# Four pre-normalised layers on one core: output projection woven into the last pair of heads, group means taken off X for good

## Chip, core and metric

The kernel is one program on one core of a Trainium2 chip. The metric is the device time of one execution, in microseconds (us). Everything is computed in float32.

## What is computed

X has 512 channels of 64 x 64 pixels (4096). Four layers follow one another, each reading the group-normalised X (32 groups of 16 channels, no scale or shift) and adding its result to X itself:

```python
x = x + L0(gn(x)); x = x + L1(gn(x)); x = x + L2(gn(x)); x = x + L3(gn(x))
def gn(v):                 # per group of 16 channels, over channels and pixels
    return (v - mean) / sqrt(var + 1e-5)
def L0(f):                 # 8 heads of 64 channels, all 4096 x 4096 scores
    q, k, v = (conv1x1(f, w / sqrt(512)) for w in (wq, wk, wv))
    sim = -(|q_i|^2 + |q_j|^2 - 2 q_i.k_j) / 8
    return conv1x1(softmax(sim) @ v, wo / sqrt(512))
def L1(f):                 # L2 is the same with other weights
    pwa, abc = split(conv1x1(f, w_in) + b_in, [128])   # 128 and 896 channels
    dw0, dw1, dw2 = split(depthwise7x7(abc) + dw_b)    # 128, 256, 512
    h = pwa * dw0
    h = (conv1x1(h, pw0) + b) * dw1
    h = (conv1x1(h, pw1) + b) * dw2
    return conv1x1(h, w_out) + b_out
def L3(f):                 # linear attention
    qkv0 = conv1x1(f, w_qkv) * s_qkv + b_qkv           # 768 channels
    agg = affine(depthwise5x5(qkv0))
    q, k, v = split(concat(qkv0, agg)); q, k = relu(q) + eps, relu(k) + eps
    y = (v k^T) q / (mean(k).q + eps) * g_norm + bt_norm + v
    return conv1x1(y, w_proj) * s_proj + b_proj
```

## The kernel before

X stays in SBUF all through, as four chunks of 128 channels (c = 0 to 3), and the 4096 pixels are worked on in eight blocks of 512 columns (b or k). The kernel issues its instructions through a framework that orders them per engine from its own estimates of time; each engine then runs its own list in order, with semaphores between the engines. In the convolution layers the matmuls (`pc.matmul`, line 579) keep the order in which they are written.

**Group parameters.** `_group_params` (L91) turns the per-block statistics (`bn_stats`) into mean and 1/std: four `bn_aggr` (L96), a small matmul with `gmask` (L98) that averages over a group, a copy of the mean (L100), three small operations, a second matmul (L107), Sqrt on ScalarE (L111), and five more small operations on VectorE that end in `gn_r` (L119).

**L0, `_attention_pairs`.** `_normalize` (L315) rewrites X as (X - mean) / std with 32 VectorE operations (L326), one per chunk and block. Then the heads go in four pairs. `project` makes Q, K and V of a pair (L394, L405). For each block of queries, 32 steps t follow: `scores` (four matmuls on quarters of the array, then two Exp on ScalarE), and, two steps behind, `values` (four matmuls) and an addition to `acc` on VectorE (L500). `close` divides a finished block by its sums (L462 to L475) and overwrites Q of that pair with the result; it is issued inside the next block at t = 3. All PSUM products except `av` rotate through three buffers (`ps_s`).

**The check and the output projection, `_attention`.** The kernel checks that all softmax sums were in range (`good`, `one`, `okay`, L510 to L513), every engine loads that value into a register (L524), and a branch (L525) skips a long general form of the attention, which does not run with these inputs. Since X was overwritten by its normalised form, the output projection loads the original X again (`xin`, L538), multiplies by `wo` (256 matmul instructions, L542; each fp32 matmul counts as two), adds (L545) and takes the statistics of the next layer (L548).

**L1 and L2, `_gated_convs`.** The weights are multiplied by 1/std in place (`scaled`, L740). The mean is not taken off X: the first time that a weight tile is used (`k == 0`), `taking` multiplies it with the mean as well (L761, `ps_m`, a product one column wide), and the result is taken off the bias (`b_in`, L764). Each product goes through VectorE into a zero-padded `plane` (L771) and from there, by a DMA that ScalarE triggers (L603), to DRAM (`F`), from where the depthwise convolution loads it shifted (`S`, L629).

**L3, `_linear_attention`.** It treats the mean in the same way (L963, `b_qkv`, L966 and L967); here ScalarE writes the plane (L970) and triggers the DMA.

Of the kernel before, what the change touches and what calls it, by code (L numbers as in the profile page):

```python
# [10 lines left out]
FP = mybir.dt.float32  # L11
# [5 lines left out]
P = 128  # L17
# [72 lines left out]

def _group_params(nc, small, psum, stats, gmask):  # L91


    mv = small.tile([P, NC, 2], FP, tag="gn_mv", name="gn_mv")
    for c in range(NC):
        nc.vector.bn_aggr(mv[:, c, :], stats[:, c, :, :].rearrange("p b s -> p (b s)"))  # L96
    ps = psum.tile([P, BLK], FP, tag="mm", name="gn_ps")
    nc.tensor.matmul(ps[:, 0:NC], gmask, mv[:, :, 0], start=True, stop=True)  # L98
    mean = small.tile([P, NC], FP, tag="gn_mean", name="gn_mean")
    nc.vector.tensor_copy(mean, ps[:, 0:NC])  # L100

    d = small.tile([P, NC], FP, tag="gn_d", name="gn_d")
    nc.vector.tensor_sub(d, mv[:, :, 0], mean)
    nc.vector.tensor_mul(d, d, d)
    nc.vector.tensor_add(d, d, mv[:, :, 1])
    ps = psum.tile([P, BLK], FP, tag="mm", name="gn_ps")
    nc.tensor.matmul(ps[:, 0:NC], gmask, d, start=True, stop=True)  # L107
    a = small.tile([P, NC], FP, tag="gn_a", name="gn_a")
    nc.vector.tensor_scalar(a, ps[:, 0:NC], GN_EPS, None, ALU.add)  # L109
    s = small.tile([P, NC], FP, tag="gn_s", name="gn_s")  # L110
    nc.scalar.activation(s, a, AF.Sqrt)  # L111
    r = small.tile([P, NC], FP, tag="gn_r", name="gn_r")
    nc.vector.reciprocal(r, s)

    t = small.tile([P, NC], FP, tag="gn_t", name="gn_t")
    nc.vector.tensor_mul(t, r, r)
    nc.vector.tensor_mul(t, t, a)
    nc.vector.tensor_scalar(t, t, -0.5, 1.5, ALU.mult, ALU.add)
    nc.vector.tensor_mul(r, r, t)  # L119
    return mean, r  # L120
# [3 lines left out]
def trunk_kernel(ctx: ExitStack, tc: tile.TileContext, a: dict, out: bass.AP):  # L124
# [42 lines left out]
    def new_stats():  # L167
        return small.tile([P, NC, NB, 6], FP, tag="stats", name="stats")

    dram = ctx.enter_context(tc.tile_pool(name="dram", bufs=1, space=bass.MemoryType.DRAM))  # L170
    F = [dram.tile([P, FORM.planes, FORM.plane], FP, tag=f"F{i}", name=f"F{i}") for i in range(NDW)]
# [5 lines left out]

    stats = _attention(tc, a, X, vcol, ident, gmask, neg2, small, new_stats)
    stats = _gated_convs(tc, a, X, vcol, gmask, small, new_stats, stats, F)
    _linear_attention(tc, a, X, vcol, vall, ident, gmask, small, stats, F3, Z, out)  # L180


# [131 lines left out]

def _normalize(tc, X, gmask, small, psum, new_stats):  # L315

    nc = tc.nc
    st = new_stats()
    for b in range(NB):
# [14 lines left out]

def _attention_pairs(tc, a, X, QO, gmask, small, new_stats, okay):

# [11 lines left out]
    scale = D ** -0.5  # L348
    gain_in = 1.0 / math.sqrt(C)
    NT = N // P  # L350
# [3 lines left out]
    with tc.tile_pool(name="att1", bufs=1) as p1, tc.tile_pool(  # L354
# [10 lines left out]

        ps_mm = _Halves()
        _normalize(tc, X, gmask, small, ps_mm, new_stats)


# [12 lines left out]
        def project(pair):  # L382
            w = p1.tile([P, 3, NC, P], FP, tag="wqkv", name=f"wqkv{pair}")
            nc.sync.dma_start(out=w, in_=a["L0_wqkv"][pair])
            Q = QO[pair]
            sq = []
            for b in range(NB):
                cols = ts(b, BLK)
                if b % 2 == 0:
                    sq.append(ptp.tile([P, 2 * BLK], FP, tag="pt", name="sq"))  # L390
# [71 lines left out]
        def close(pair, b, av, acc):  # L462
# [12 lines left out]
            nc.vector.scalar_tensor_tensor(good, rd, 1.0 / SUM_LOW, good, ALU.is_le, ALU.mult)  # L475

        for pair in range(HEADS // 2):
            project(pair)
            done = None
            for b in range(NB):  # L480
# [23 lines left out]
                nc.vector.tensor_add(avs, avs, av[1])  # L504
                done = (pair, b, avs, acc)
            close(*done)


# [6 lines left out]

def _attention(tc, a, X, vcol, ident, gmask, neg2, small, new_stats):

    nc = tc.nc
    gain_out = 1.0 / math.sqrt(C)
    opool = tc.alloc_tile_pool(name="opool", bufs=1, side="right")  # L520
    O = [opool.tile([P, N], FP, tag=f"O{i}", name=f"O{i}") for i in range(NC)]
    okay = small.tile([1, 1], mybir.dt.int32, tag="okay", name="okay")
    _attention_pairs(tc, a, X, O, gmask, small, new_stats, okay)
    found = nc.values_load(okay[0:1, 0:1])  # L524
    with tc.If(found < 1):  # L525
        _attention_general(tc, a, X, O, ident, neg2)

    stats = new_stats()
    with tc.tile_pool(name="wo", bufs=1, side="right") as wop, tc.tile_pool(
        name="xin", bufs=2, side="right"  # L530
    ) as xinp, tc.tile_pool(name="ps_o", bufs=4, space=PSUM) as ps_o:
        wo = wop.tile([P, NC, C], FP, tag="wo", name="wo")
        nc.scalar.dma_start(out=wo, in_=a["L0_wo"])
        for b in range(NB):
            cols = ts(b, BLK)
            xin = xinp.tile([P, NC, BLK], FP, tag="xin", name="xin")
            for c in range(NC):
                nc.sync.dma_start(out=xin[:, c, :], in_=a["x"][c, :, cols])  # L538
            for o in range(NC):
                ps = ps_o.tile([P, BLK], FP, tag="o", name="ps_o")  # L540
                for c in range(NC):
                    nc.tensor.matmul(  # L542
                        ps, wo[:, c, ts(o, P)], O[c][:, cols], start=(c == 0), stop=(c == NC - 1)
                    )
                nc.vector.scalar_tensor_tensor(  # L545
                    X[:, o, cols], ps, gain_out, xin[:, o, :], ALU.mult, ALU.add
                )
                nc.vector.bn_stats(stats[:, o, b, :], X[:, o, cols])  # L548
    opool.release()
    return stats  # L550
# [155 lines left out]
@with_exitstack  # L706
def _gated_convs(ctx, tc, a, X, vcol, gmask, small, new_stats, stats, F):

# [11 lines left out]
    for layer in ("L1", "L2"):  # L720
# [13 lines left out]
        nc.sync.dma_start(out=pw1, in_=a[f"{layer}_pw1"])  # L734
        mean, rstd = _group_params(nc, small, ps_mm, stats, gmask)
        stats = new_stats()
        b_in = small.tile([P, 8], FP, tag="b_in", name="b_in")

# [13 lines left out]

        def taking(w, i, k):


            ps = product(lambda c: w[:, c, :], [pc.pixels(X[:, c, :], k) for c in range(NC)])
            if k == 0:
                pm = ps_mm.tile([P, BLK], FP, tag="mm", name="ps_m")
                for c in range(NC):
                    pc.matmul(  # L760
                        pm[:, 0:1], w[:, c, :], mean[:, c : c + 1],  # L761
                        start=(c == 0), stop=(c == NC - 1),
                    )
                nc.vector.tensor_sub(b_in[:, i : i + 1], vcol(pre + "b_in", i), pm[:, 0:1])  # L764
            return ps

        def fused(i, k):

            pc.take(
                i, k, taking(w_in[i], 1 + i, k),  # L770
                lambda dst, src: nc.vector.tensor_scalar(  # L771
                    dst, src, b_in[:, 1 + i : 2 + i], None, ALU.add
                ),
# [6 lines left out]
        def gate(i, b):  # L780

            h = [D[c][:, ts(b, BLK)] for c in range(min(i, 3))]
            if i == 0:
                ps = taking(w_gate, 0, b)
                bias = b_in[:, 0:1]
            elif i < 3:
# [73 lines left out]
@with_exitstack  # L860
def _linear_attention(ctx, tc, a, X, vcol, vall, ident, gmask, small, stats, F, Z, out):

# [48 lines left out]
    with ExitStack() as st:  # L911
# [25 lines left out]

        mean, rstd = _group_params(nc, small, ps_mm, stats, gmask)

        def product(w, hs):  # L940
# [3 lines left out]
            return ps  # L944

        b_qkv = wp.tile([P, NQKV], FP, tag="b_qkv", name="b_qkv")

# [6 lines left out]
        def fused(i, k):  # L954

            w = w_qkv[i]
            ps = product(lambda c: w[:, c, :], [pc.pixels(X[:, c, :], k) for c in range(NC)])
            bias = b_qkv[:, i : i + 1]
            if k == 0:
                pm = ps_mm.tile([P, BLK], FP, tag="mm", name="ps_m")  # L960
                for c in range(NC):
                    pc.matmul(
                        pm[:, 0:1], w[:, c, :], mean[:, c : c + 1],  # L963
                        start=(c == 0), stop=(c == NC - 1),
                    )
                nc.vector.tensor_mul(bias, pm[:, 0:1], vcol(pre + "s_qkv", i))  # L966
                nc.vector.tensor_sub(bias, vcol(pre + "b_qkv", i), bias)  # L967
            pc.take(
                i, k, ps,
                lambda dst, src: nc.scalar.activation(  # L970
                    dst, src, AF.Identity, bias=bias, scale=vcol(pre + "s_qkv", i)
                ),
# [95 lines left out]
        def added():  # L1068
# [10 lines left out]
            nc.vector.tensor_mul(pbias, ps[:, 0:NC], vall(pre + "s_proj"))  # L1079
            nc.vector.tensor_add(pbias, pbias, vall(pre + "b_proj"))  # L1080


# [195 lines left out]
```

## Time and profile before

| | us |
|---|---|
| median of 3 runs | 3992.67 (3990.71 to 3994.23) |
| the profiled execution, its own time | 3995.15 |
| its span in the profile | 3993.1 |
| TensorE (PE) busy | 3896.0 |
| VectorE (DVE) busy | 2268.5 |
| ScalarE (ACT) busy | 1823.8 |
| GpSimd (POOL) busy | 66.7 |

A line of the profile names the source line, the engine, the operation, the tile written and the tile read, and how often it ran. PEld is the loading of weights into the array. "Idle before" is the time in which the engine stood still just before, with the engine or DMA that ended the wait. Start times are counted from the start of the span; 2.05 us of the execution lie outside it.

### The profile page before, as it was taken

How to read it: one execution, taken by the hardware profiler on the slowest of the kernel's cores; microseconds unless marked ns; L12 is line 12 of the kernel's file. 1: busy time of each engine (PE TensorE's matmuls, PEld its weight loads, DVE VectorE, ACT ScalarE, POOL GpSimd, SP SyncE). 2: the span in 40 equal slices, each digit the busy share in tenths (PEclk: the TensorE clock that was granted, in tenths of full speed). 3: DMA queues.
4: the chain of work that ended last, by engine and by line, in shares of the span. 5: the costliest groups of instructions: out<-in, count | busy, mean ns of one | idle time of the engine just before them, and what ended most of it. 6: DMA issues, size and time to landing. Idle time of an engine off the chain costs nothing. (4 is left out here: it accounts for less than half of the span.)

```text
span 3993.1 us, 81533 instructions
## 1 busy us (share of the span) xinstructions
PE 3896.0 (98%) x35842; PEld 1766.7 (44%) x35842; DVE 2268.5 (57%) x2497; ACT 1823.8 (46%) x2599; POOL 66.7 (2%) x67
## 2 busy tenths in 40 slices
PE   6999999999999999999998999999999999989999
PEld 4533346333353333543332445554455544445544
DVE  4677763777727777457776323466434664233335
ACT  0677753777717777357775024441144520222210
POOL 0000000000000000000000000000000000001110
PEclk9999999999999999999999999999999999989999
DMA  2000000000000000000000235551255511686234
GB/s 93 9 1 1 1 1 9 1 1 1 1 9 1 1 1 1 1 1 1 1 1 24 95 129 158 174 146 43 90 149 176 158 45 56 177 208 139 74 89 144
DMA packets 243097, 241.26 MB, mean 60 GB/s; under 512 B 15384, under 2 KB 204056, under 8 KB 242480
## 3 DMA queue, kind: packets, MB, share of 16 engines
q1 hardware_dynamic: 215920, 176.16, 16.4%
q10 hardware_dynamic: 26784, 59.76, 4.1%
q8 instruction: 284, 4.65, 0.5%
q14 instruction: 77, 0.63, 0.1%
q0 software_dynamic: 32, 0.06, 0.0%
HBM read 176.15 MB, written 59.77 MB: 59 GB/s over the span
## 5 line engine op out<-in xcount | busy, mean ns | idle before, releaser
L447 ACT ACTIVATE pt<-ps_s,A 128x512 f32<-128x512 f32 x2048 | 1286.7, 687 | 470.0 <-PE ps_s L439 451.6
L500 DVE TENSOR_TENSOR acc<-acc,pt 128x1024 f32<-128x1024 f32 x960 | 1174.3, 1223 | 334.3 <-ACT pt L447 308.3
L457 PE MATMUL av<-pt,V 64*64 64x512 f32 x8192 | 1116.5, 590 | 0.9 <-ACT pt L447 0.9
L439 PE MATMUL ps_s<-O,K 64*64 64x512 f32 x8192 | 1115.2, 589 | 0.0
L457 PEld LDWEIGHTS av<-pt,V 64*64 64x64 f32 x8192 | 343.0, 133 | 551.0 <-issue 509.7
L439 PEld LDWEIGHTS ps_s<-O,K 64*64 64x64 f32 x8192 | 338.7, 133 | 545.6 <-issue 286.2
L635 ACT COPY S<-S 32x1295 f32<-32x1295 f32 x224 | 284.2, 1269 | 353.1 <-DMA S<-F 285.9
L579 PE MATMUL ps<-X,w_in_L 128*128 128x512 f32 x896 | 407.0, 604 | 4.6 <-DVE w_in_L L740 4.6
L579 PE MATMUL ps_cv<-S,T 64*32 64x128 f32 x13824 | 242.5, 278 | 16.8 <-DMA S<-G 15.0
L579 PEld LDWEIGHTS ps_cv<-S,T 64*32 64x32 f32 x13824 | 199.5, 107 | 122.5 <-issue 80.8
L579 PEld LDWEIGHTS ps<-X,w_in_L 128*128 128x128 f32 x896 | 165.5, 191 | 197.2 <-issue 194.8
L771 DVE TENSOR_SCALAR plane<-ps,b_in 128x512 f32<-128x512 f32 x112 | 83.8, 748 | 263.7 <-PE ps L579 210.7
L394 PE MATMUL ps_qk<-X,wqkv 128*128 128x512 f32 x512 | 227.7, 598 | 2.1 <-DVE X L326 2.1
L579 PE MATMUL ps<-h,w_out_L 128*128 128x512 f32 x512 | 227.9, 598 | 0.0
L579 PE MATMUL ps<-X,w_qkv 128*128 128x512 f32 x384 | 172.7, 606 | 3.2 <-DVE w_qkv L949 3.2
L579 PE MATMUL ps<-h,pw_L 128*128 128x512 f32 x320 | 146.7, 610 | 7.4 <-DVE X L809 6.2
L398 ACT ACTIVATE O<-ps_qk 128x512 f32<-128x512 f32 x32 | 19.1, 597 | 277.5 <-PE ps_qk L394 277.5
L394 PEld LDWEIGHTS ps_qk<-X,wqkv 128*128 128x128 f32 x512 | 95.7, 192 | 113.1 <-issue 109.4
L579 PEld LDWEIGHTS ps<-h,w_out_L 128*128 128x128 f32 x512 | 95.0, 190 | 114.6 <-issue 106.5
L111 ACT ACTIVATE gn_s<-gn_a 128x4 f32<-128x4 f32 x4 | 0.8, 205 | 304.8 <-DVE gn_a L109 304.8
L830 ACT ACTIVATE h<-h,vec 128x1024 f32<-128x1024 f32 x56 | 63.0, 1147 | 154.6 <-DVE h L695 154.3
L689 DVE STREAM_TRANSPOSE h<-ps_cv 128x512 f32<-128x512 f32 x112 | 109.0, 1045 | 38.4 <-PE ps_cv L579 38.4
(130 smaller groups left out, 2486.4 us busy)
## 6 DMA issues: line engine op xcount, KB each, us to landing
T<-in_L_T_dram SPq DMA_DIRECT2D x112, 384.0 KB, 4.2
F<-plane ACTq DMA_DIRECT2D x112, 324.0 KB, 2.9
S<-F SPq DMA_DIRECT2D x224, 162.0 KB, 4.3
S<-G SPq DMA_DIRECT2D x192, 136.0 KB, 4.1
row<-G SPq DMA_DIRECT2D x80, 272.0 KB, 4.0
G<-plane ACTq DMA_DIRECT2D x48, 289.0 KB, 2.5
T<-in_L_T_dram SPq DMA_DIRECT2D x48, 256.0 KB, 4.2
xin<-in_x_dram SPq DMA_DIRECT2D x32, 256.0 KB, 3.7
```

Of the source, the lines that this page charges most:

```text
L111: nc.scalar.activation(s, a, AF.Sqrt)
L394: nc.tensor.matmul(ps, w[:, n, c, :], X[:, c, cols], start=(c == 0), stop=(c == NC - 1))
L398: nc.scalar.activation(Q[:, cols], ps, AF.Copy, scale=2 * scale * gain_in)
L439: nc.tensor.matmul(ps[ts(half, D), ts(h, BLK)], K[rows, t * P + half * D : t * P + (half + 1) * D], QO[pair][rows, cols], start=True, stop ...
L447: nc.scalar.activation(pt[:, ts(h, BLK)], ps[:, ts(h, BLK)], AF.Exp, bias=A[:, t, h : h + 1])
L457: nc.tensor.matmul(av[half][rows, :], V[keys, t, rows], pt[keys, ts(h, BLK)], start=(t == 0), stop=(t == NT - 1),)
L500: nc.vector.tensor_add(acc, acc, pt)
L579: self.tc.keep_in_program_order(self.nc.tensor.matmul(*args, **kw))
L635: nc.scalar.copy(flat[ts(2 * rho + 1, 32), 0:n], flat[ts(2 * rho, 32), f.bx : f.bx + n])
L689: nc.vector.transpose(out, src)
L771: lambda dst, src: nc.vector.tensor_scalar(dst, src, b_in[:, 1 + i : 2 + i], None, ALU.add),
L830: nc.scalar.activation(t, t, AF.Identity, bias=vcol(pre + "dw_b", i))
```

## The change

The means are now subtracted from X itself, in place and for good. A new object, `_Centered`, holds `less` (the negated mean) and `offset` (the sum of all means taken off so far), and hands out the subtractions ("takes"): when the mean is known, the four chunks of block 0 go to ScalarE (two) and GpSimd (two); the other 28 go to VectorE and ScalarE in L0, to ScalarE in L1 and L2, to VectorE in L3. `offset` is added back with `pbias` in L3. In return, the one-column products with the mean and the bias corrections are gone; in L0 the 1/std goes into the weights (`wqkv`), as it already does in the other layers, and the rewriting of X by `_normalize` is gone from the path that runs.

X now still holds the residual branch, so it is not loaded again. The output projection moves ahead of the check: within the last pair, after block b, the four products of block b - 1 are issued (`output`), and those of the last two blocks around and after the last `close`. Its weights are loaded at the start of the last pair, into the tile of `wqkv` and a fourth one. The branch now stands directly ahead of L1, and the general form behind it reloads X and has its own normalisation and projection.

```diff
 def _group_params(nc, small, psum, stats, gmask, known=None):
     nc.vector.tensor_copy(mean, ps[:, 0:NC])
+    if known is not None:
+        known(mean)
...
+class _Centered:
+    def first(self, view):
+        def known(mean):
+            self.less = self.small.tile([P, NC], FP, tag="less", name="less")
+            self.nc.vector.tensor_scalar(self.less, mean, -1.0, None, ALU.mult)
+            for c in range(NC):
+                self.take(view(c), c, self.nc.gpsimd if c > 1 else self.nc.scalar)
+            self.nc.vector.tensor_add(self.offset, self.offset, mean)
+        return known
+    def take(self, xs, c, eng):
+        less = self.less[:, c : c + 1]
+        if eng is self.nc.scalar:
+            eng.activation(xs, xs, AF.Identity, bias=less)
+        else:
+            eng.tensor_scalar(xs, xs, less, None, ALU.add)
...
 def _attention_pairs(...):
-        _normalize(tc, X, gmask, small, ps_mm, new_stats)
+        for b in range(NB):
+            for c in range(NC):
+                nc.vector.bn_stats(stats[:, c, b, :], X[:, c, ts(b, BLK)])
+        _, rstd = _group_params(
+            nc, small, ps_mm, stats, gmask, centered.first(lambda c: X[:, c, 0:BLK])
+        )
...
             nc.sync.dma_start(out=w, in_=a["L0_wqkv"][pair])
+            for n in range(3):
+                eng = nc.vector if (pair, n) == (0, 0) else nc.gpsimd
+                eng.tensor_tensor(
+                    w[:, n], w[:, n], rstd.unsqueeze(2).to_broadcast([P, NC, P]), ALU.mult
+                )
             for b in range(NB):
+                if pair == 0 and b:
+                    for c in range(NC):
+                        centered.take(X[:, c, cols], c, nc.scalar if c > 1 else nc.vector)
...
+        def output(b, chunks):
+            for o in chunks:
+                ps = ps_mm.tile([P, BLK], FP, tag="mm", name="ps_o")
+                for c in range(NC):
+                    nc.tensor.matmul(
+                        ps, wo[o][:, c, :], QO[c][:, cols], start=(c == 0), stop=(c == NC - 1)
+                    )
+                xs = X[:, o, cols]
+                nc.vector.scalar_tensor_tensor(xs, ps, gain_out, xs, ALU.mult, ALU.add)
+                nc.vector.bn_stats(stats[:, o, b, :], xs)
...
                 done = (pair, b, avs, acc)
+                if pair == HEADS // 2 - 1 and 0 < b < NB - 1:
+                    output(b - 1, range(NC))
+            if pair == HEADS // 2 - 1:
+                output(NB - 2, range(2))
             close(*done)
+        output(NB - 2, range(2, NC))
+        output(NB - 1, range(NC))
...
 def _gated_convs(...):
-        mean, rstd = _group_params(nc, small, ps_mm, stats, gmask)
+        _, rstd = _group_params(
+            nc, small, ps_mm, stats, gmask, centered.first(lambda c: pc.pixels(X[:, c, :], 0))
+        )
-            if k == 0:
-                pm = ps_mm.tile([P, BLK], FP, tag="mm", name="ps_m")
-                for c in range(NC):
-                    pc.matmul(
-                        pm[:, 0:1], w[:, c, :], mean[:, c : c + 1],
-                        start=(c == 0), stop=(c == NC - 1),
-                    )
-                nc.vector.tensor_sub(b_in[:, i : i + 1], vcol(pre + "b_in", i), pm[:, 0:1])
         def fused(i, k):
+            if i == 0 and k:
+                for c in range(NC):
+                    centered.take(pc.pixels(X[:, c, :], k), c, nc.scalar)
...
 def _linear_attention(...):
         def fused(i, k):
+            if i == 0 and k:
+                for c in range(NC):
+                    centered.take(pc.pixels(X[:, c, :], k), c, nc.vector)
-            bias = b_qkv[:, i : i + 1]
-            if k == 0:
-                pm = ps_mm.tile([P, BLK], FP, tag="mm", name="ps_m")
...
-                nc.vector.tensor_mul(bias, pm[:, 0:1], vcol(pre + "s_qkv", i))
-                nc.vector.tensor_sub(bias, vcol(pre + "b_qkv", i), bias)
...
+            nc.vector.tensor_add(pbias, pbias, centered.offset)
```

## Prediction

> **What bounds the kernel now.** I read the page first: busy shares, and the span in 40 slices.
>
> ```profile
> PE 3896.0 (98%) x35842; PEld 1766.7 (44%) x35842; DVE 2268.5 (57%) x2497; ACT 1823.8 (46%) x2599; POOL 66.7 (2%) x67
> PE   6999999999999999999998999999999999989999
> ```
>
> TensorE works nearly all the time, and only some 97 us are left in which it stands still. So the change can win in two ways: by taking work off TensorE, or by shortening its few gaps. The table by stretches shows the gaps; its columns are the length, then busy time and (instructions) of PE, PEld, DVE, ACT and POOL, granted clock, DMA share and GB/s.
>
> ```profile
> 0.00:32.24 32.24, 1.14 (x4) 1.00 (x4) 24.26 (x54) 1.49 (x2) 2.20 (x10) 1.00 0.79 287
> 32.24:2175.30 2143.06, 2141.64 (x18172) 890.95 (x18172) 1449.34 (x1250) 1345.45 (x2144) 0.00 (x0) 1.00 0.01 2
> 2175.30:2194.76 19.46, 1.27 (x7) 0.37 (x7) 6.79 (x8) 1.87 (x2) 0.00 (x0) 0.63 0.28 96
> 2194.76:2307.95 113.19, 113.18 (x256) 49.66 (x256) 44.08 (x65) 0.00 (x0) 0.00 (x0) 0.97 0.25 88
> 2307.95:2314.01 6.06, 0.95 (x4) 0.83 (x5) 4.09 (x14) 0.20 (x1) 1.82 (x3) 0.68 0.72 246
> 2314.01:2825.00 510.99, 505.70 (x6368) 254.24 (x6368) 257.48 (x336) 173.63 (x140) 6.86 (x7) 0.99 0.43 125
> 3338.86:3345.95 7.09, 1.04 (x5) 0.91 (x5) 4.39 (x20) 0.20 (x1) 2.78 (x5) 0.65 0.79 297
> ```
>
> Within the attention (second line) PE has 1.4 us of idle time in 2143, so what is put in there costs its full PE time. The gap of 19.5 us behind it and the 6 us ahead of L1 are what the moved projection can touch. The timeline shows what fills them:
>
> ```profile
> 2183.09 0.15 DVE L513 TENSOR_SCALAR okay<-ps_ok 1x1 int32<-1x1 f32 x1 [0.37 <-PE ps_ok L512]
> 2187.52 7.45 SPq L538 DMA_DIRECT2D xin<-in_x_dram  x8
> 2194.76 10.61 PE L542 MATMUL ps_o<-O,wo 128*128 128x512 f32 x17 [11.71 <-DMA wo<-in_L_wo_dram]
> 2319.01 0.95 PE L579 MATMUL ps_m<-gn_mean,w_in_L 128*128 128x1 f32 x8
> 2319.82 27.71 PE L579 MATMUL ps<-X,w_in_L 128*128 128x512 f32 x64
> 31.64 14.69 DVE L326 TENSOR_SCALAR X<-X,gn_mean,gn_r 128x512 f32<-128x512 f32 x32
> 32.24 9.43 PE L394 MATMUL ps_qk<-X,wqkv 128*128 128x512 f32 x16 [2.08 <-DVE X L326]
> ```
>
> From `okay` (end 2183.24) to the first instruction behind the branch (2187.52) pass 4.3 us, and then `wo` must still land. A `ps_m` group holds PE for 0.81 us (2319.01 to 2319.82), and a normalisation takes DVE 14.69 / 32 = 0.46 us.
>
> **Part 1: the `ps_m` products go.** The groups table has 112 + 16 + 48 = 176 such instructions, so 22 groups of 8. At 0.81 us that is 17.8 us of PE time, all of it between other matmuls. L1 has PE busy for 505.7 of 511 us, so 8 groups a layer convert in full. The six of L3 stand ahead of a stretch (3545 to 3590) in which PE is busy for only 31 of 45 us behind DMAs; if all six were lost there, 16 x 0.81 = 13.0 us remain. Upper end: the groups' busy time, 13.3 + 1.9 + 5.7 = 20.9. I take **-17.8**, since that stretch begins when PE's last product is out and so moves with it.
>
> **Part 2: the takes in the steady course cost nothing.** In L1 and L2, 28 takes go to ACT, four per block, at 0.63 us (its SBUF-to-SBUF row, L401, mean 629 ns) to 0.69 (Exp with a bias pointer, L447): 2.5 to 2.8 us, where PE needs 3.44 us per block (planes written at 2323.53, 2326.97). They cover what is queued behind them, the triggers of `F<-plane`: the changed program's order has 14 takes right after the Sqrt, then trigger 0, four takes, trigger 1, and so on, so X runs three and a half blocks ahead. The 14 last 8.8 us from the Sqrt, and plane 0 is ready 8.0 us after it (2.0 to PE's start, 5.16 for the cold first product, 0.8 for the plane), so trigger 0 is late by under 1 us, where the same plane buffer is wanted again only 6.9 us later and the write takes 2.9. In L3 the 17 takes behind the weight scaling need 7.8 us of an idle DVE. In L0 GpSimd scales 11 weight tiles at 1.1 us, a pair ahead. Without cover, 56 takes x 0.63 = 35 us would show.
>
> **Part 3: the layer starts get longer.** Every chain gets `less` and `offset`, 0.20 us each by the spacing of its small rows. In L0 and L3 there is more: the program's order puts takes between the small steps of the chain on DVE, ahead of the weight scaling on which PE waits. L0 has 12 of them there. One hides behind the second matmul (0.68 us wait), 0.27 us behind the Sqrt, so (12 - 1) x 0.46 - 0.27 = 4.8 us; the scaling (0.69, and 0.1 to PE) replaces a normalisation ahead of PE's start, which adds 0.2. Sum: 0.4 + 4.8 + 0.2 = **+5.4**. L3 has 11: (11 - 1) x 0.46 - 0.27 + 0.4 = 4.7, less 0.92 us in which the scaling waited for its weights anyway: **+3.8**. L2 has none: **+0.4**. GpSimd's first takes have no row; its tensor_tensor rows of the same size (1.04 to 1.27 us) put chunk 3 at 2.8 us behind the mean, where PE wants it 8 us behind it in L0 and L3, and 4 us in L2. Bounds for the three together: +6 (takes at half price) to +13.
>
> **Part 4: the projection moves.** Before, from the last `values` to L1's first product: 2314.01 - 2175.30 = 138.7 us. After, the same PE work is: 256 x 0.4287 = 109.7 (steady spacing; the 113.2 of before holds a cold start, 10.6 us for 17 instructions), `ps_d` 1.0, and a new gap G from the last product to L1. G by rows: eviction 0.73 and `okay` 0.15; `bn_stats` stands ahead of DVE's own load of `okay` (0.7); branch 4.2 to 4.3 (DVE arrives at 5.2 to 5.8); four `bn_aggr`, none hidden any more, 1.05; the matmul and mean copy 0.9, so the mean at 7.2 to 7.8; then `less`, two takes on ACT (1.2 us), a table load of 1.28, Sqrt, five small steps, scaling: 4.75. G = 12.0 to 12.6, taken 12.5. The weights of L1, loaded during the projection before, are now issued behind the branch, at about 5.6; they landed 4.2 to 6.3 us after issue elsewhere, so at 9.8 to 11.9, while the scaling wants them at 11.5: a tie. Sum 109.7 + 1.0 + 12.5 = 123.2: **-15.5**. G's bounds: 9 (the register load runs ahead of `bn_stats`, table load hidden) to 19 (the old gap again).
>
> Interleaving itself I cost at nothing, against a bound of 2 us (an Exp pair of 1.27 and an eviction of 0.73) at each of six places, 12 us. A product waits for a PSUM buffer used three allocations earlier, which is evicted by then; the scores behind `output` wait for buffers that DVE frees within 0.73 us, while two score steps (1.7 us) come first. DVE has 64 more operations of 0.69 us: per block 39 + 5.4 + 0.7 + 5.5 = 51 us against PE's 55 + 13.7. A gain is excluded there, since PE had no idle time. In the tail, `close` needs a reciprocal of 3.35, and two products (6.9 us) cover it; without them PE would wait about 5 us.
>
> [...]
>
> **Sum:** -17.8 + 5.4 + 0.4 + 3.8 - 15.5 = **-23.7 us** on the profiled execution: 3995.15 becomes 3971.4. That execution is 2.5 us above the median of the runs, so the median becomes 3992.67 - 23.7 = **3969.0**.
>
> **Rivals.**
> *The boundary gives less.* The branch, the late weights and the restarts eat the move: G = 19 and 6 us of the stalls make it 12.5 us worse: 3981. For it: no row shows a branch with a layer start right behind it. Against: each step of G has a row.
> *The `ps_m` time doesn't convert* beyond half, and the starts cost 13: -8.9 + 13 - 15.5 = -11.4: 3981. With the rival above as well, 3994: no change. Against: L1's 98.9% of busy PE.
> *Slower: ACT paces the start of L1 and L2.* If the takes of a block stood behind the trigger of the block ahead, each of 7 blocks would add its takes and the plane, 2.5 + 0.8, 23 us a layer and 46 in all: 3969 + 46 = 4015. It decides when a take lasts over 3.44 / 4 = 0.86 us, or X runs under one block ahead; to be slower than before by 0.2% the takes must lose 23.7 + 8 = 32 us, 32 / 56 = 0.57 us each beyond that, so 1.43 us a take. Against: ACT's rows say 0.63 to 0.69, and the order runs ahead.
> *It doesn't do what it says:* the projection would end up behind the last pair all the same. The program's order excludes this: sixteen `ps_o` matmuls stand at the end of each of six blocks.
>
> **Numbers.** 0.2% of this kernel is 8 us, about what its measurement can tell from no change. Chances: the forecast with its sizes (3961 to 3976) 0.70; the boundary or the conversion falling short (3976 to 3984) 0.19, still faster; both short, no change 0.07; slower 0.04. Faster is 0.89. The 80% range takes the favourable ends (G = 9, starts +6, so 7 us better) down to 3962, and 11 us of the shortfalls up to 3980.
>
> **What would show it.** No `ps_m` rows, and about 505.7 - 6.5 us of PE in L1; PE's first product of L0 at about 37.6 us instead of 32.24, with takes between the `gn_` rows on DVE; L3's start about 3.8 us longer than 7.09; one gap of about 12.5 us between the last `ps_o` and L1; in the last pair no idle PE at the six places. The prediction is wrong if that gap exceeds 20 us, if PE waits on `X L345` in L1 or L2, or if scores wait on DVE behind `ps_o`.

## The result, and the profile after

| | before | after |
|---|---|---|
| median, us | 3993.77 (3990.71 to 3994.71) | 3967.76 (3965.61 to 3976.42) |
| ratio | | 0.9941 (95%: 0.9928 to 0.9954) |
| profiled execution, its span | 3995.15, 3993.1 | 3972.97, 3971.3 |

The change makes the kernel faster by 0.59%, 23.6 us by the ratio and 26.0 by the medians. The forecast was 3969.0.

The engine row of the page after shows where the work went: PE has 15.8 us less, ACT 48 more, GpSimd (POOL) 29 more.

```profile
PE 3880.2 (98%) x35666; PEld 1732.5 (44%) x35666; DVE 2276.4 (57%) x2490; ACT 1871.9 (47%) x2678; POOL 95.6 (2%) x86
```

The same table by stretches as before (length, busy time of PE, PEld, DVE, ACT, POOL, granted clock, DMA share, GB/s). The gap of 19.5 us in mid-span is gone. One of 13.6 us stands ahead of L1. The start of L0 has become longer, 36.05 instead of 32.24, and that of L3 too, 10.05 instead of 7.09.

```profile
0.00:36.05 36.05, 1.15 (x5) 1.03 (x5) 30.12 (x69) 8.86 (x13) 7.09 (x13) 1.00 0.73 264
36.05:2263.75 2227.70, 2226.29 (x18364) 912.55 (x18364) 1473.35 (x1269) 1347.16 (x2151) 13.04 (x11) 1.00 0.01 3
2263.75:2292.75 29.00, 29.00 (x74) 12.28 (x70) 15.91 (x22) 0.58 (x1) 0.00 (x0) 1.00 0.00 0
2292.75:2306.33 13.58, 1.18 (x7) 1.03 (x5) 6.05 (x20) 5.81 (x10) 6.04 (x6) 0.68 0.48 154
3322.77:3332.82 10.05, 0.95 (x6) 0.83 (x5) 9.66 (x34) 1.54 (x3) 6.97 (x7) 0.62 0.57 210
```

Two places of the timeline explain these starts. In L0, the takes stand on DVE between the small steps of the group norm, and four of those that run beside GpSimd's takes last 0.82 to 0.89 us instead of 0.48. PE's first product follows behind the weight scaling (L427):

```profile
28.46 0.48 DVE L347 TENSOR_SCALAR X<-X,less 128x512 f32<-128x512 f32 x1
28.93 0.84 DVE L347 TENSOR_SCALAR X<-X,less 128x512 f32<-128x512 f32 x1
29.77 0.89 DVE L347 TENSOR_SCALAR X<-X,less 128x512 f32<-128x512 f32 x1
35.26 0.68 DVE L427 TENSOR_TENSOR wqkv<-wqkv,gn_r 128x512 f32<-128x512 f32 x1
36.05 4.61 PE L442 MATMUL ps_qk<-X,wqkv 128*128 128x512 f32 x5 [5.56 <-issue]
```

Ahead of L1, 4.8 us pass between the end of `okay` (2293.47) and the first `bn_aggr`, and the scaling of the weights takes DVE 1.50 us:

```profile
2293.34 0.13 DVE L585 TENSOR_SCALAR okay<-ps_ok 1x1 int32<-1x1 f32 x1
2298.24 1.06 DVE L96 BATCH_NORM_AGGREGATE gn_mv<-stats 128x2 f32<-128x48 f32 x4 [4.09 <-DVEq L598]
2304.64 3.48 POOL L819 TENSOR_TENSOR w_in_L<-w_in_L,gn_r 128x512 f32<-128x512 f32 x3 [1.00 <-DMA w_gate_L<-in_L_w_in_dram]
2304.72 1.50 DVE L819 TENSOR_TENSOR w_in_L<-w_in_L,gn_r 128x512 f32<-128x512 f32 x1 [0.31 <-DMA w_gate_L<-in_L_w_in_dram]
2306.33 10.05 PE L657 MATMUL ps<-X,w_in_L 128*128 128x512 f32 x17 [4.38 <-DMA pw_L<-in_L_pw_dram]
```

Below, a stage runs from its first product to the first product of the next; the table puts the profiled executions side by side (us).

| run | start of L0 | L0 to L1 | L1 to L2 | L2 to L3 | L3 to end |
|---|---|---|---|---|---|
| before | 32.24 | 2281.77 | 515.44 | 516.50 | 647.15 |
| before again (e11) | 31.48 | 2281.06 | 514.74 | 519.36 | 645.26 |
| after | 36.05 | 2270.28 | 511.20 | 515.29 | 638.48 |
| after again (e1) | 35.82 | 2268.77 | 507.75 | 511.77 | 638.69 |
| before, no `ps_m` (e2) | 31.45 | 2284.00 | 509.54 | 511.42 | 637.49 |
| late takes (e3) | 33.80 | 2270.35 | 508.82 | 512.19 | 636.04 |
| one stretch (e4) | 35.86 | 2267.51 | 507.35 | 511.65 | 639.73 |
| no fallback (e5) | 36.27 | 2264.25 | 507.72 | 511.68 | 639.58 |
| double takes (e6) | 35.64 | 2270.06 | 515.92 | 522.54 | 640.94 |
| busy gap (e7) | 36.06 | 2269.91 | 506.18 | 510.93 | 638.32 |
| projection behind (e8) | 35.66 | 2281.15 | 509.59 | 513.72 | 636.88 |
| all four edits (e9) | 33.15 | 2266.71 | 508.37 | 506.62 | 635.25 |
| GpSimd behind (e10) | 35.95 | 2269.20 | 509.24 | 515.12 | 640.99 |

### The profile page after: what moved, and what is told of

The parts are those of the page before. It is cut to its first block, busy times and chain, and to the rows that moved or that the text cites. A ratio compares the mean times of both kernels' runs of the same rounds, so it can differ in the third digit from the quotient of the medians.

```text
span 3971.3 us, 81238 instructions
## 1 busy us (share of the span) xinstructions
PE 3880.2 (98%) x35666; PEld 1732.5 (44%) x35666; DVE 2276.4 (57%) x2490; ACT 1871.9 (47%) x2678; POOL 95.6 (2%) x86
## 5 line engine op out<-in xcount | busy, mean ns | idle before, releaser
L843 DVE TENSOR_SCALAR plane<-ps,vec 128x512 f32<-128x512 f32 x112 | 83.4, 748 | 301.2 <-PE ps L657 230.4
L767 DVE STREAM_TRANSPOSE turned<-ps_cv 128x512 f32<-128x512 f32 x48 | 31.6, 697 | 226.6 <-PE ps_cv L657 226.6
L345 ACT ACTIVATE X<-X,less 128x512 f32<-128x512 f32 x78 | 49.5, 708 | 230.1 <-DVE less L335 218.5
L865 DVE SCALAR_TENSOR_TENSOR h<-ps,vec,h 128x512 f32<-128x512 f32 x112 | 82.4, 745 | 104.7 <-PE ps L657 101.4
```

What stands on the lines that cost most here:

```text
L345: eng.activation(xs, xs, AF.Identity, bias=less)
L767: nc.vector.transpose(out, src)
L843: lambda dst, src: nc.vector.tensor_scalar(dst, src, vcol(pre + "b_in", 1 + i), None, ALU.add),
L865: nc.vector.scalar_tensor_tensor(d, ps, bias, d, ALU.add, ALU.mult)
```

## The experiments

My theory was the sum of the prediction, and three things in the trace disagreed with it by some microseconds: the projection's stage gave less, L3 gave more, and L1 and L2 did not shrink alike. The runs take the parts one by one.

**e1, e11: both kernels again, unedited.**

> The changed kernel once more, unedited, as the yardstick of this group. Expected: 3968 us, 23 to 27 below the kernel before, and in its profile the same milestones as in the first profile (first product of L0 at 36.05 us, of L1 at 2306, of L2 at 2817.5, of L3 at 3333) to within half a microsecond. Rival: if the milestones wander by 2 us or more from one execution to the next, the differences between the terms of the sum and the trace (some 4 us in the projection and 4 us in L3) are scatter and need no explanation.

> The kernel before once more, unedited, one look for the spread of its stages between executions. Theory (L3 shrank by 8.7 us where the products explain 4.9, because the first profile of the kernel before had PE at half clock for some 3.5 us more in L3 than the others): L3 now 641 to 645 us long instead of 647.2, the attention to L1 unchanged at 2282 within 1 us. Rival (L3 of the kernel before is 647 us long in every execution, and the products are worth more there): 646 to 648.

Measured: e1 3968.58 us (ratio 0.9931, 0.9918 to 0.9945), e11 3993.98. The milestones of e1 agree for L0 (35.82) and differ by 1.7 us at L1, 5.2 at L2 and 8.7 at L3, so its rival is right for the lengths of L1 and L2, but not for the two stages that it names: L3 repeats within 0.2 us and the stage up to L1 within 1.5. The same program has L1 3.5 us shorter, with PE busy for 498.28 us instead of 501.90. The table by stretches shows where, at 2720 to 2736, behind a PE gap of 3.1 us that both executions have; the column ahead of the last two is the granted clock. After, first execution:

```profile
2720.00:2728.00 8.00, 4.90 (x9) 1.94 (x8) 7.17 (x9) 4.53 (x4) 0.00 (x0) 0.78 0.19 56
2728.00:2736.00 8.00, 8.00 (x16) 3.44 (x15) 2.78 (x4) 0.00 (x0) 0.00 (x0) 0.80 0.00 0
```

The same program, e1:

```profile
2720.00:2728.00 8.00, 4.90 (x13) 2.23 (x13) 6.38 (x9) 3.70 (x4) 0.00 (x0) 1.00 0.11 33
2728.00:2736.00 8.00, 8.00 (x20) 3.59 (x19) 3.47 (x5) 0.00 (x0) 0.00 (x0) 1.00 0.00 0
```

The clock costs 8 x (0.22 + 0.20) = 3.4 us in one execution and nothing in the other; these rows hold eight PE instructions fewer in the first, at 0.43 us each. Differences of up to that size in one stage of one profile are no effect of an edit. In L0, too, the start differs: the first weight loads (PEld) follow at 0.85 us instead of 0.43 for 5.5 us behind the first product in the first profile and for 3.0 in e1, and half of the 2.5 us between them is 1.3 of the 1.5 us up to L1. The L3 of e11 is 645.3, just outside the theory's 641 to 645; the rival's 646 to 648 misses it too.

**e2: the first part alone,** the kernel before without the mean's products.

```diff
-            if k == 0:
-                pm = ps_mm.tile([P, BLK], FP, tag="mm", name="ps_m")
-                ...
-                nc.vector.tensor_sub(b_in[:, i : i + 1], vcol(pre + "b_in", i), pm[:, 0:1])
...
-                    dst, src, b_in[:, 1 + i : 2 + i], None, ALU.add
+                    dst, src, vcol(pre + "b_in", 1 + i), None, ALU.add
```

> The kernel before, without the ps_m products and the bias made of them (the mean's part of the bias in L1 to L3 is left out of the computation; nothing takes its place). This is the first part of the change alone. Theory (22 groups of 0.81 us on PE's path): 17.8 us less than before, 13.0 to 20.9, so 3973 to 3981. Rival (the groups lie in PE's idle time, before a convolution that waits for its transfers anyway): 9 us or less, 3985 or more.

Measured: 3974.78 against 3995.55, 20.8 us less by the medians, at the upper end of the expected 13.0 to 20.9 (ratio 0.9944, 0.9930 to 0.9957, so 22.4 by the ratio). Against the mean of the two profiles before, L1 is 5.6 us shorter, L2 6.5 and L3 8.7. So the products lay on PE's path nearly everywhere, and the rival (half) is out. L1 and L2 fit 8 x 0.81 = 6.5; L3 gives more than 6 x 0.81 = 4.9.

**e3: the takes out of the group norm's chain,** by a second copy of the negated means that depends on rstd.

```diff
+    def settle(self, r):
+        self.rest = self.small.tile([P, NC], FP, tag="rest", name="rest")
+        self.nc.vector.scalar_tensor_tensor(self.rest, r, 0.0, self.less, ALU.mult, ALU.add)
```

> The changed kernel, with the takes of the later blocks in L0 and L3 reading a second copy of the negated means that is made from rstd (times 0, plus the means), so that the scheduler cannot put them into the chain of the group norm. Theory (the 12 and 11 DVE takes inside the chain cost 4.5 us in L0 and about 4 in L3, and PE's start moves by all of it): first product of L0 at 32 to 32.5 instead of 36.05, start of L3 3.5 to 4 earlier against the end of L2, 6 to 8 us less than the changed kernel in all. Rival (the delay is given back later: the takes then hold up the evictions of the first blocks, or L3's convolutions wait for their transfers in any case): PE starts earlier, but the time falls by 3 us or less.

Measured: 3962.95 us (ratio 0.9918, 0.9905 to 0.9932), 5.6 under e1, less than the expected 6 to 8 and more than the rival's 3; the two intervals overlap, so the starts in the trace carry the verdict. L0 starts at 33.80, which is 2.0 earlier than e1, not 3.5; and L3 7.5 us behind L2's last product instead of 10.05. The timeline of e3 shows what holds each of them next. In L0, GpSimd's scaling now starts together with DVE's, and DVE's takes 1.55 us instead of 0.68; in L3, DVE waits 0.69 us for the landing of the weights.

```profile
32.11 2.48 POOL L433 TENSOR_TENSOR wqkv<-wqkv,gn_r 128x512 f32<-128x512 f32 x2 [0.74 <-DVE gn_r L121]
32.14 1.55 DVE L433 TENSOR_TENSOR wqkv<-wqkv,gn_r 128x512 f32<-128x512 f32 x1
33.80 10.06 PE L448 MATMUL ps_qk<-X,wqkv 128*128 128x512 f32 x16 [4.19 <-issue]
```

```profile
3324.32 0.69 DVE L1029 TENSOR_TENSOR w_qkv<-w_qkv,gn_r 128x512 f32<-128x512 f32 x1 [0.69 <-DMA w_qkv<-in_L_w_qkv_dram]
3325.16 11.32 PE L663 MATMUL ps<-X,w_qkv 128*128 128x512 f32 x20 [3.22 <-DVE w_qkv L1029]
```

So the takes' place in the order costs 2.0 + 2.6 = 4.6 us by these two starts, and the 5 to 6 us of the medians agree. In this one profile L0's 2.0 us don't all arrive: at L1's first product e3 is 0.4 us ahead of e1 (2304.15 and 2304.59). Its weight loads follow at 0.85 us for 6.0 us behind the first product and those of e1 for 3.0, which gives back 1.5.

**e10: GpSimd's scaling behind VectorE's,** for which GpSimd reads a copy of rstd made from DVE's scaled weights (in L0 likewise).

```diff
         scaled(w_in[0], nc.vector)
+        again = small.tile([P, NC], FP, tag="again", name="again")
+        nc.vector.scalar_tensor_tensor(again, w_in[0][:, :, 0], 0.0, rstd, ALU.mult, ALU.add)
+        rstd = again
```

> The changed kernel with only the copy of rstd behind VectorE's own scaling in L0 to L2, one look for the trace. Theory (VectorE's scaling of L1's first weights lasts 1.50 us because GpSimd's starts within 0.1 us of it, against 0.69 in L2): 0.69 in L1 too, and L1's first product 0.8 us earlier behind rstd. Rival (the 1.50 us come from the weights still landing in L1): 1.5 again.

```profile
2304.36 0.69 DVE L826 TENSOR_TENSOR w_in_L<-w_in_L,gn_r 128x512 f32<-128x512 f32 x1 [0.31 <-DMA w_in_L<-in_L_w_in_dram]
```

The 1.50 us become 0.69, with the wait for the weights (0.31) as before, and L1's first product follows 1.10 us behind rstd instead of 1.92. So the cause was GpSimd beside DVE, and not the weights. Its single time (3972.17) can't tell 0.8 us.

**e4, e8: the projection in one stretch, and behind the branch again.**

```diff
-                if pair == HEADS // 2 - 1 and 0 < b < NB - 1:
-                    output(b - 1, range(NC))
             if pair == HEADS // 2 - 1:
+                for b in range(NB - 2):
+                    output(b, range(NC))
                 output(NB - 2, range(2))
```

The edit of e8, in `_attention`, with `output` taken out of `_attention_pairs`:

```diff
+    with tc.tile_pool(name="wo", bufs=1, side="right") as wop, tc.tile_pool(
+        name="ps_o", bufs=4, space=PSUM
+    ) as ps_o:
+        nc.scalar.dma_start(out=wo, in_=a["L0_wo"])
+        ...
+                nc.vector.scalar_tensor_tensor(xs, ps, gain_out, xs, ALU.mult, ALU.add)
+                nc.vector.bn_stats(stats[:, o, b, :], xs)
```

> The changed kernel, with the first six blocks of the output projection not woven into the last pair's loop but done in one stretch behind its last product of values; the rest (in place into X, last block behind the last close) stays. Theory (weaving by itself hides nothing, since PE is the bound there: the gain of this part comes from what was between the attention and L1): 0 to 3 us less than the changed kernel, because the six gaps at the places of insertion (about 2.4 us) go too. Rival (the weaving is what hides the weights' loading, the evictions on DVE and the branch): 5 to 15 us more.

> The changed kernel with the move of the output projection undone: all eight blocks stand behind the branch again, with their weights loaded there on ACT's queue, but still in place into X, without the loads of x that the kernel before had. Theory (from the last product of values to L1 the changed kernel needs 127 us with the woven blocks, the old order 19.5 of gap, 113 of projection and 6.6 of gap before L1): 10 to 14 us more than the changed kernel, 3978 to 3982, and a second stretch of half clock on PE at the projection's start. Rival (the gap of the old order was made by the loads of x alone, so it shrinks without them): 5 us more or less.

Measured: e4 3963.80 (0.9919, 0.9905 to 0.9932), 4.8 under e1 where 0 to 3 were expected, and in the trace 1.3 us less up to L1. The interval overlaps that of e1, so all that the times can say is that weaving gains nothing. The trace says a little more: the stretch with the six blocks is 2.1 us shorter than in e1. e8 gives 3976.23 (0.9955, 0.9942 to 0.9969), 7.7 us above e1 by the medians, 9.6 by the ratios and 12.4 by the stage up to L1, below or in the expected 10 to 14. Its stage is 2281.15 us long, as in the kernel before (2281.77), although it loads no x: the gap of some 19 us there is made by the check, the branch and the landing of `wo`; the timeline has PE idle for 10.91 us behind `ps_ok`, and the landing of `wo`, issued behind the branch, ends it.

```profile
2197.14 112.02 PE L593 MATMUL ps_o<-O,wo 128*128 128x512 f32 x256 [10.91 <-DMA wo<-in_L_wo_dram]
```

What the move gains, then, is that one of two stops of PE goes, not that products hide beside the attention. One rival is not tested: some 5.6 us of that stop are the landing of `wo` (by before: issued at 2189.20, first product at 2194.76), and loading it ahead of the branch, with the products left behind it, might have gained a part of the 12 us without the move.

**e5: no fallback** (the register load, the branch and the general path are left out).

```diff
-    found = nc.values_load(okay[0:1, 0:1])
-    with tc.If(found < 1):
-        ...
```

> The changed kernel without the register load, the branch and the general path behind it (left out: the fallback for sums out of range; on these inputs it is not taken). Theory (of the 13.6 us between the last ps_o and L1's first product, 4.8 are the load and the branch, which the short gap before L2, 6.6 us, doesn't have): the gap falls to 7 to 9 us, 5 to 7 us less than the changed kernel. Rival (the gap is set by the weights of L1, whose space only comes free at the end of the attention, and by the table load of the Sqrt): gap 11 or more, under 3 us less.

Measured: 3962.36 (0.9920, 0.9905 to 0.9935), 6.2 under e1, with intervals that overlap. The last `bn_aggr` follows 0.7 us behind `okay`, and L1's first product stands 7.8 us behind the last `ps_o`, as expected. Of the 5.9 us that go from the gap, 5.0 lie between `okay` and the mean; 0.8 come from DVE's scaling, which takes 0.69 us here. The rows of e5:

```profile
2293.39 0.14 DVE L585 TENSOR_SCALAR okay<-ps_ok 1x1 int32<-1x1 f32 x1
2294.24 0.37 DVE L96 BATCH_NORM_AGGREGATE gn_mv<-stats 128x2 f32<-128x48 f32 x1
2300.52 9.90 PE L627 MATMUL ps<-X,w_in_L 128*128 128x512 f32 x18 [3.74 <-DVE w_in_L L789]
```

**e6: the takes in L1 and L2 doubled.**

```diff
+                    xs = pc.pixels(X[:, c, :], k)
+                    centered.take(xs, c, nc.scalar)
+                    nc.scalar.activation(xs, xs, AF.Identity, bias=centered.none)
```

> The changed kernel, with every ACT take of the later blocks in L1 and L2 followed by a second one of zero (28 more ACTIVATEs of 0.62 us a layer). Theory (a block of PE lasts 3.44 us and four takes 2.5, so the takes cost nothing as they are; doubled they last 5.0 a block and pace PE from about the fourth block): first stage of L1 and of L2 longer by 5 to 11 us each, 10 to 22 in all. Rival (ACT's triggers and the planes already pace these blocks): 17 us or more in each, 35 in all. Second rival (X runs so far ahead that it hides this too): under 3 us in all.

Measured: 3986.30 (0.9971, 0.9959 to 0.9983), 17.7 above e1; L1 8.2 and L2 10.8 us longer, as the theory has it. From the fourth block PE waits for ACT ahead of each four instructions:

```profile
2320.86 1.98 PE L659 MATMUL ps<-X,w_in_L 128*128 128x512 f32 x4 [0.25 <-ACT X L844]
2323.30 1.98 PE L659 MATMUL ps<-X,w_in_L 128*128 128x512 f32 x4 [0.46 <-ACT X L844]
```

**e7: PE kept busy in the gaps.** The products of `gmask` add work that nobody reads.

```diff
+            ps = psum.tile([P, BLK], FP, tag="mm", name="ps_w")
+            for _ in range(n):
+                nc.tensor.matmul(ps, gmask, src, start=True, stop=True)
```

> The changed kernel with products of the group mask whose result nobody reads put into PE's gaps before L2 and L3 (2 before the product for the mean, 1 between the two products of the group norm, 2 behind the second), and 2 behind the second before L1. Theory (PE's granted clock falls to 0.50 in these gaps and stays there for 4 to 6 us of each layer's first products, which loses 2 to 3 us a layer): granted clock 1.00 at the first product of L2 and L3, L2 and L3 each 2 to 3 us shorter, L1 0 to 2: 4 to 8 us less than the changed kernel. Rival (the clock falls in these gaps whatever PE does, or the added products delay the group norm's chain by as much): within 2 us of the changed kernel.

Measured: 3964.99 (0.9922, 0.9908 to 0.9935), 3.6 under e1, below the expected 4 to 8, and the two intervals overlap, so the table of the clock has to carry the verdict. The first 3 us of L2's products, first after (two rows), then e7:

```profile
2817.53:2820.53 3.00, 3.00 (x4) 1.45 (x5) 0.00 (x0) 3.00 (x6) 3.00 (x4) 0.50 0.02 5
2820.53:2823.53 3.00, 3.00 (x5) 1.04 (x5) 0.00 (x0) 1.18 (x2) 1.74 (x2) 0.52 0.00 0
```

```profile
2812.15:2815.15 3.00, 3.00 (x7) 1.41 (x8) 0.00 (x0) 3.00 (x6) 3.00 (x4) 1.00 0.00 0
```

After, L2's first 6 us run at 0.50; in e7 the clock is 1.00 from the first product of L1 and of L2, and PE does 7 instructions in the 3 us that held 4. In L3 it failed: there the takes between the steps still left PE idle for 3.58 us behind the last added product, and the clock was 0.50 for the first 5.5 us again.

**e9: all four edits** (e3, e4, e7 and e10).

> Four edits on the changed kernel at once: the late takes, the busy gaps, the projection in one stretch, and in L0 to L2 a copy of rstd made behind VectorE's own scaling of the first weights, so that GpSimd's scaling starts behind it. Theory (2.0 + 2.6 from the late takes, 1.5 + 3 + 3 from the clock at the starts of L1, L2 and L3, the last now that L3's chain is short enough, 0.8 + 0.8 from the scaling, 1.3 from the one stretch): 14 to 16 us less than the changed kernel, 3952 to 3955. Rival (they overlap: a shorter chain leaves PE waiting for the weights of L1 and L3): 6 to 10 less, 3958 to 3962.

Measured: 3951.78 us (3951.33 to 3952.14; ratio 0.9894, 0.9879 to 0.9909), 16.8 under e1 by the medians, 14.8 by the ratios: the theory's 14 to 16. This version beats both kernels. L0 starts at 33.15, with DVE's scaling at 0.68 us, and L3, where e7 alone had failed, starts at a clock of 1.00 with a gap that e3 has shortened to 1.58 us. L2 starts at 1.00 too; L1 still has 0.50 for its first 1.5 us. The rows of e9:

```profile
32.37 0.68 DVE L445 TENSOR_TENSOR wqkv<-wqkv,gn_r 128x512 f32<-128x512 f32 x1
3314.85 5.39 PE L681 MATMUL ps<-X,w_qkv 128*128 128x512 f32 x12 [1.58 <-DVE w_qkv L1054]
```

## Why the prediction was right

The total was right (-23.7 forecast, -23.6 by the ratio), but partly because errors of both signs cancelled. Means of two profiles on each side, against the sum:

| step | forecast | measured |
|---|---|---|
| start of L0 | +5.4 | +4.1 |
| to L1 (part 4) | -15.5 | -11.9 |
| L1 and start of L2 | -6.5 + 0.4 | -5.6 |
| L2 and start of L3 | -6.5 + 3.8 | -4.4 |
| L3 | -4.9 | -7.6 |
| sum | -23.7 | -25.4 |

(The forecast's 22 x 0.81 = 17.8 is split here over the layers, 8, 8 and 6 groups, and rounded.)

*Part 1, the products.* Right: e2 has 20.8 us by the medians for a forecast of 17.8, just inside its upper bound of 20.9. The term that was too small is L3's: 4.9 forecast, 8.7 in e2. Both profiles of before have a granted clock of 0.96 in L3's fourth 40 us, a loss of 1.6 us that after and e2 don't have there (e1 has it 40 us later). The rest, about 2 us, stays open: no run took L3's products alone. A candidate that wasn't tested is the bias made of these products, which e2 leaves out as well: before, ACT waits 21.5 us in all for `b_qkv` (L967) ahead of L3's planes.

*Part 2, the takes on ACT cost nothing.* Right: in e1 PE waits 6.9 us in all ahead of the products of X and `w_in`, none of it put down to takes, and e6 shows that the cover is not large. The first profile of after does put 2.4 us, at L2's start, down to a take (`ACT X L345`), which the prediction had named as a sign of being wrong. But the scaling of the weights ends there at 2817.38, the take at 2817.42 and the product starts at 2817.53, so the take can have cost no more than 0.04 us. At 1.24 us a pair of takes, over the price of 0.86 at which ACT starts to pace PE, the layers become 8 to 11 us longer. The slower rival named the right mechanism, and e6 is consistent with its threshold; its price of 23 us a layer was too high, since X ran ahead.

*Part 3, the starts.* Right in kind, too high in L0 (5.4 against 4.1) and in L3 (3.8 against 3.0 by the gap, 10.05 - 7.08); L2's gap grew by 0.5 for a forecast of 0.4. A part of L0's distance is scatter, as the chain itself began earlier in the profiles of after (26.1 us by the means instead of 26.6): from the first `bn_aggr` to PE's first product it is 9.79 us in after and 5.26 before, 4.5 more. Two sizes were wrong and worked against each other. Four takes beside GpSimd's cost 0.82 to 0.89, not 0.46; and in L0 the Sqrt has a table load ahead of it, so that DVE waits 1.25 us there (shown in e3, where nothing fills that wait) and not 0.27, and more of the takes hid. I had counted that table load in L1 and not in L0's cover.

*Part 4, the projection.* The step that failed: 15.5 forecast, 11.5 in the first profile and 13 in e1, and 12.4 when e8 undoes it. Three terms make up most of the first profile's 4.0 us. The gap G is 13.64, not 12.5. Up to the mean its rows were right: 7.5 us behind the last product, where the forecast has 7.2 to 7.8. From the mean to L1's first product the forecast has 4.75 and the trace 6.1: 0.8 of this is DVE's scaling beside GpSimd, which e10 takes away, and 0.3 the wait for the weights, which the forecast called a tie. The six insertions cost 2.1 us and not nothing: a block with one lasts 70.19 us instead of 56.10, so 14.09 for products that last 13.73 in e4's one stretch. The tail has 0.4 more. The place was right in e5: without the branch the gap falls to 7.8.

*The table loads.* The trace after has a table load in L1's chain: ACT's takes end at 2301.82, the load (1.28 us) starts at 2301.84 and the Sqrt at 2303.14, 1.30 us later. In L0 the load starts at 29.80 and the Sqrt at 31.09, 1.29 us later, and in before the first Exp stands 1.29 us behind the start of its load. So the 1.28 us that part 4 has for it was right.

```profile
121.83 1.28 ACT L447 ACT_TABLE_LOAD   x1 [9.21 <-DVE A L429]
123.12 2.42 ACT L447 ACTIVATE pt<-ps_s,A 128x512 f32<-128x512 f32 x4
```

*What the sum did not have at all* is PE's clock. Every start of L1, L2 and L3 in before and after runs its first products at 0.50: for 3.0 us in L1 of before, 5.1 in after, 4.1 in e1, 3.3 in e4. Half of that is lost: the weight loads of L2 in after follow each other at 0.85 us up to 2822.78, and at 0.43 from 2823.53 on. The clock is the largest cause of the scatter that I found: as an estimate, half of PE's busy time in the stretches recorded at 0.50 is 27.0 us in the first profile of after and 20.3 in e1, and with the 1.3 us of L0's start that is 8.0 of the 8.5 us between the two spans. With that half taken off each stage, the two profiles agree within 0.4 us in L1 and L2, and against before L1 is shorter by 6.4 us (forecast 6.1), L2 by 3.8 (2.7) and L3, where PE also waits for transfers at 0.50 and the estimate is rough, by 6.7 (4.9). e7 and e9 show that the loss at most layer starts can be avoided.

## What to carry to other kernels

When a correction is moved from matmuls to the operand, look for its price at the layer starts (here 4.1 us in L0 and 3.0 in L3), and in the instruction order for operations that a scheduler puts between the small dependent steps of a chain, and bind them to the chain's last result. Moving the products ahead of a stop gained the stop here (12.4 us, e8), not the products; weaving them into a stage with a busy PE gained nothing (one stretch, e4, is 1.3 us shorter up to L1). Where PE stands still for a few microseconds ahead of a layer, count the half-clock products behind the gap as well (here 3.0 to 6.0 us of them at each start of L1, L2 and L3 in before and after), and read two profiles of one program before explaining 3 us of a stage.

## What the runs showed of the hardware

- *PE's clock behind a gap.* With PE idle for 3.58 us ahead of L3 (e7) the granted clock was 0.50 afterwards, with 1.58 (e9) it stayed 1.00, and a gap of 3.1 us in L1 had both outcomes in two executions of one program (after, e1); what decides between them was not shown. In before, after, e1 to e6 and e8 the products behind the gap ahead of L1, L2 and L3 run at 0.50 for 3.0 to 6.2 us, in L1 of e9 for 1.5; in L1 and L2 of e7 and in L2 and L3 of e9 they run at 1.00 from the first. Inside the span every recorded stretch at 0.50, in all thirteen traces, lasts a whole multiple of 3.41 us, one to eleven (in after, 2724.42 to 2731.25 is two and 2813.17 to 2823.41 three), and in before and in after the stretches at 1.00 between them do so too. In L0's start the profile's clock column says 1.00 while weight loads follow each other at 0.85 us instead of 0.43 up to 41.5 us (after); the first entry of the trace's clock record is at 41.55, so ahead of it the column says nothing.
- *VectorE beside GpSimd.* A tensor_tensor of 128x512 on DVE takes 0.69 us, and 1.50 to 1.55 when GpSimd's starts within 0.1 us before it (after, e3); with GpSimd's ordered behind it, 0.68 to 0.69 (e9, e10). GpSimd's own takes 1.04 us undisturbed (e10), and where DVE's starts 0.2 us ahead of it, DVE's takes 0.69 and GpSimd's 1.39 to 1.40 (L2 of after, L1 and L3 of before). Not settled: in L0 and L3 of after GpSimd's is recorded 0.23 and 0.18 us ahead, and yet DVE's takes 0.68 and GpSimd's 1.76 to 1.81. Why the two lengthen each other was not shown.
- *GpSimd's takes* last 1.56 to 1.59 us each in L1 and L2 of after, and 1.86 to 1.98 beside DVE's in L0 and L3; the profile has 13.9 us for all eight.
